# Entering values of the last state-space chunk as TensorE products with diagonal matrices

## The chip, the cores and the metric

The kernel runs on one core of a Trainium2 chip. A core has a matrix engine (TensorE, written PE in the profile; PEld is its loading of weights), a vector engine (VectorE, DVE), a scalar engine for activation functions (ScalarE, ACT), a general engine (GpSimd, POOL) and a sync engine (SP), which here issues the DMAs. Each engine works through its own queue in order, and the queues wait for each other on semaphores. SBUF is the working memory of 128 partitions. PSUM is the matrix engine's output memory, with eight banks of 128 x 512 fp32 values. The metric is the device time of one execution in microseconds (us), as the median of several runs.

## The reference

The model is a sequence of four residual layers on x of shape (2, 1024, 256): attention with ALiBi, a feed-forward layer with ternary weights, a Mamba state space, and a feed-forward layer that keeps two of every four values. The change concerns the state space, with 512 channels d, 16 states n and 128 values of low rank:

```python
x_conv = silu(conv1d(x))                       # (b, l, 512)
x_dbl = x_conv @ x_proj_weight.T               # dt_low (128), Bm (16), Cm (16)
delta = softplus(dt_low @ dt_proj_weight.T + dt_proj_bias)
deltaA = exp(einsum('bld,dn->lbdn', delta, A))
dBu = einsum('bld,bln,bld->lbdn', delta, Bm, x_conv)
h = dA * h + dbu                               # for each time l in turn
y = einsum('bdn,bn->bd', h, c)                 # then y + x_conv * D, times silu(z)
```

All values are fp32. The state h of every pair (d, n) runs through the whole sequence.

## The kernel before

Time is cut into four chunks of 512 steps, two for each of the two batch elements. A chunk goes through attention, then through the rest: `ternary_ffn`, `state_space` and `kept_two_ffn`. Python generators interleave the attention of one chunk with the rest of the chunk before it, in shares that weights after each `yield` set. The rest of the last chunk (k = 3, `tail_end` in the code) has no attention beside it and stands alone at the end. The order inside an engine's queue is made from this program by the framework's scheduler, which may move an instruction past others that do not depend on it; the tile pools add the waits for buffers that are used again.

In `state_space` a tile has 128 channels on the partitions and 512 time steps. There are four blocks of channels (c) and 16 states (n), so 64 products (c, n) per chunk. Before them, `in_proj` and the convolution make `xs`, the products `bcp` (line 531) give the 32 rows of B and C, which go through DRAM (`bcd`, line 538), and `dtl` (line 541) gives the low-rank part of delta. The input weights and these temporaries lie in the pool `mi`, which is closed before the pool `m2` of the 64 products is opened in its place.

`steps(c)` (line 552) makes delta (`dl`) and `du = delta * xs` for a block: a product `dt` on PE, Abs, Exp and Ln on ACT, `sv`, `sr` and `dl` on DVE, `sl` and `du` on POOL. It runs ahead of the loop for block 0 and in the middle of each block for the next one. The loop is a software pipeline, written as a list of stages, each with a lag (line 655). For a product i the stages are:

- `ask_b`, `ask_c` (line 582): a DMA on SP's queue spreads row n of B or C over 128 partitions (`bs`, `cs`, 256 KB each).
- `enter` (line 602): `db = du * bs`. In the last chunk DVE does this for the n that three does not divide, POOL for the others; in other chunks POOL does all.
- `decay` (line 608): `da = exp(delta * A)` on ACT. In the last chunk it goes to the two PSUM banks `s`, which attention has left free.
- `scan` (line 613): the recurrence over 512 steps on DVE, from `da`, `db` and the carried state.
- `weigh` (line 627): `hc = hs * cs` on POOL.
- `total` (line 632): four transposes by PE add hc to the bank `y` of the block; the first n adds the skip term `sk`. After the last n, `gate` (line 643) copies y, transposes it back and multiplies it by silu(z).

PSUM has two banks `s`, three `mm`, one `y` and two `r`. After the loop the out-projection `mo` (line 674) adds to x, and `kept_two_ffn` follows.

## Time and profile before

| | |
|---|---|
| median of 3 runs | 2002.48 us (2001.0 to 2005.09) |
| profiled execution, its own time | 1999.44 us |
| its span | 1997.7 us |
| busy PE, DVE, ACT, POOL | 1732.6, 1283.2, 947.2, 850.8 us |
| bytes moved by DMA | 272.73 MB |
| first scan of the last chunk starts | 1782.1 us |
| last hc of the last chunk ends | 1923.8 us |

The span is one execution from its first to its last instruction; the time of that execution lies 1.7 us above it. A group of instructions in the profile names the line, engine and operation, the tile written and the tiles read, the shape and the count; then its busy time in us and the mean of one in ns; then the idle time of the engine just before these instructions, and what ended most of it. The `[...]` in a timeline is the same for one entry. PEclk is the clock granted to PE, as a share of full speed. Matrix products are pipelined: the duration of one holds its filling and draining, and the distance between two in a row is shorter.

### The profile page before, as it was taken

What the parts mean: (1) busy time and instruction counts of PE and PEld (TensorE: products, weight loads), DVE (VectorE), ACT (ScalarE), POOL (GpSimd) and SP (SyncE); (2) the same over time, 40 slices, a digit from 0 to 9 for tenths busy, and PEclk for the clock granted to TensorE, in tenths of its full rate; (3) what the DMA queues carried; (4) which work ended last, traced back from release to release, by engine and by line L of the source; (5) the groups of instructions that cost most, each with busy time, mean ns of one, the idle gap of its engine ahead of it and who ended that gap; (6) DMA issues with size and microseconds to landing.
All of it is one profiled execution on the core that took longest, in us unless ns stands there. A gap on an engine that the chain in (4) does not pass through costs nothing.

```text
span 1997.7 us, 23402 instructions
## 1 busy us (share of the span) xinstructions
PE 1732.6 (87%) x7472; PEld 1126.7 (56%) x7472; DVE 1283.2 (64%) x2397; ACT 947.2 (47%) x1713; POOL 850.8 (43%) x690
## 2 busy tenths in 40 slices
PE   6799999798989999988879999979889999764477
PEld 4466666356656566645556576546655656523344
DVE  6865455667776474468875565567877455368964
ACT  3244464555553554455653546545544363354421
POOL 5620031467792000449992004158776000449950
PEclk9899999899999999999999999989999999875569
DMA  6333342555662313246884242256663300347740
GB/s 186 96 106 106 127 151 83 157 161 193 196 199 72 108 43 124 80 146 204 253 254 151 71 140 75 84 170 198 194 197 122 116 24 14 110 144 213 234 147 11
DMA packets 187499, 272.73 MB, mean 137 GB/s; under 512 B 17248, under 2 KB 92000, under 8 KB 186352
## 3 DMA queue, kind: packets, MB, share of 16 engines
q1 hardware_dynamic: 186224, 258.65, 41.2%
q0 software_dynamic: 1152, 12.58, 1.7%
q8 instruction: 60, 0.98, 0.2%
q14 instruction: 63, 0.52, 0.1%
HBM read 248.82 MB, written 22.35 MB: 136 GB/s over the span
## 4 chain that ended last, share of the span: by engine, by line
PE 56%; DVE 18%; POOL 11%; issue 8%; DMA 4%; ACT 3%; SPq 0%; POOLq 0%; DVEq 0%; ACTq 0%
PE z L260 10%; PE s L318 7%; DVE hs L616 6%; PE pv L298 4%; PE pq L291 4%; PE pt L249 4%; PE pk L291 4%; POOL db L606 3%; DVE ss L327 3%; POOL hc L630 3%; PE o L274 3%; PE in L501 3%; PE g_g L395 3%; PE go L738 3%; PE u_g L395 3%
## 5 line engine op out<-in xcount | busy, mean ns | idle before, releaser
L630 POOL TENSOR_TENSOR hc<-hs,cs 128x512 f32<-128x512 f32 x256 | 360.3, 1419 | 74.6 <-PE y L596 67.7
L318 PE MATMUL s<-kT,qT 128*128 128x512 f32 (+3 forms) x768 | 311.4, 514 | 28.7 <-DVE ss L322 27.4
L606 POOL TENSOR_TENSOR db<-du,bs 128x512 f32<-128x512 f32 x216 | 288.2, 1346 | 47.1 <-DVE hs L616 39.0
L331 ACT ACTIVATE ss<-ss,nm 128x128 f32<-128x128 f32 (+7 forms) x256 | 198.3, 775 | 209.4 <-DVE nm L327 202.3
L322 DVE SCALAR_TENSOR_TENSOR ss<-s,lower 128x512 f32<-128x512 f32 (+3 forms) x384 | 204.4, 550 | 141.4 <-PE s L318 141.0
L260 PE MATMUL z<-pT,v 128*128 128x512 f32 (+3 forms) x768 | 264.7, 494 | 9.8 <-ACT pT L252 9.7
L611 ACT ACTIVATE da<-dl,a_neg 128x512 f32<-128x512 f32 x256 | 175.6, 689 | 183.3 <-DVE hs L616 158.9
L596 PE MATMUL y<-ident,hc 128*128 128x128 f32 x1024 | 176.2, 315 | 93.8 <-POOL hc L630 92.8
L327 DVE CUSTOM_DVE_ANT_0 ss<-ss,alibi 128x128 f32<-128x128 f32 (+7 forms) x256 | 235.5, 926 | 2.9
L249 PE MATMUL pt<-ident,ss 128*128 128x128 f32 x1152 | 186.2, 285 | 57.8 <-DVE x L280 33.7
L260 PEld LDWEIGHTS z<-pT,v 128*128 128x128 f32 x768 | 144.9, 193 | 141.0 <-issue 100.4
L252 ACT COPY pT<-pt 128x512 f32<-128x512 f32 (+3 forms) x312 | 139.4, 470 | 178.4 <-PE pt L249 176.6
L249 PEld LDWEIGHTS pt<-ident,ss 128*128 128x128 f32 x1152 | 142.9, 146 | 116.4 <-DVE x L280 47.9
L596 PEld LDWEIGHTS y<-ident,hc 128*128 128x128 f32 x1024 | 135.9, 162 | 122.4 <-POOL hc L630 120.2
L318 PEld LDWEIGHTS s<-kT,qT 128*128 128x128 f32 x768 | 135.7, 202 | 108.0 <-issue 57.2
L616 DVE TENSOR_TENSOR_SCAN hs<-da,db 128x512 f32<-128x512 f32 x128 | 153.8, 1212 | 63.1 <-POOL hc L630 27.2
L616 DVE TENSOR_TENSOR_SCAN hs<-da,carry,db 128x512 f32<-128x512 f32 x128 | 160.2, 1271 | 18.8 <-POOL hc L630 9.5
L280 DVE SCALAR_TENSOR_TENSOR x<-o,rr,x 128x256 f32<-128x256 f32 x256 | 108.7, 477 | 62.3 <-PE o L274 62.2
L298 PEld LDWEIGHTS pv<-wv,xT_a 128*128 128x128 f32 x1024 | 124.5, 192 | 35.7 <-issue 26.0
L411 POOL DMA_DIRECT2D guT<-guT_d x4 | 2.7, 675 | 303.6 <-DVE o L743 111.9
L274 PE MATMUL o<-wo,zs 128*128 128x256 f32 x512 | 124.7, 385 | 7.4 <-ACT kT L294 6.3
L298 PE MATMUL pv<-wv,xT_a 128*128 128x128 f32 x1024 | 125.6, 276 | 4.4 <-ACT zs L265 2.3
(186 smaller groups left out, 2532.9 us busy)
## 6 DMA issues: line engine op xcount, KB each, us to landing
bs<-bcd SPq DMA_DIRECT2D x256, 256.0 KB, 4.1
cs<-bcd SPq DMA_DIRECT2D x256, 256.0 KB, 4.0
alibi<-alibi_d SPq DMA_DIRECT2D x32, 512.0 KB, 4.3
wq<-in_wqT_dram SPq DMA_DIRECT2D x64, 128.0 KB, 2.6
wk<-in_wkT_dram SPq DMA_DIRECT2D x64, 128.0 KB, 2.6
wv<-in_wvT_dram SPq DMA_DIRECT2D x64, 128.0 KB, 2.6
wo<-in_woT_dram SPq DMA_DIRECT2D x64, 128.0 KB, 2.7
alibi<-alibi_d SPq DMA_DIRECT2D x32, 256.0 KB, 3.3
```

The costliest lines, as they stand in the source:

```text
L249: nc.tensor.transpose(tp[:, i, :], s[:, (kb0 + i) * P : (kb0 + i + 1) * P], ident)
L260: nc.tensor.matmul(zp[:, q0:], lhsT=st["v_all"][:, kb, :], rhs=st["pts"][kb // 4][:, kb % 4, q0:], start=(kb == 0), stop=(kb == last),)
L274: nc.tensor.matmul(op[:, i, :], lhsT=st["z"][:, (t + i) * P : (t + i + 1) * P], rhs=st["o"], start=True, stop=True,)
L298: nc.tensor.matmul(vp[:, t, :], lhsT=xT[:, c, t * P : (t + 1) * P], rhs=st["v"][:, c, :], start=(c == 0), stop=(c == KC - 1),)
L318: nc.tensor.matmul(sp[:, :n], lhsT=st["qT"][:, j * P : (j + 1) * P], rhs=st["kT"][:, k0 : k0 + n], start=True, stop=True,)
L322: nc.vector.scalar_tensor_tensor(s[:, k0 : k0 + n], sp[:, :n], CLIP, lower[:, S - W + k0 : S - W + k0 + n], op0=ALU.min, op1=ALU.max,)
L327: nc.vector.tensor_tensor_reduce(out=s[:, :W], in0=s[:, :W], in1=st["alibi"][:, :W], scale=1.0, scalar=3.0e38, op0=ALU.add, op1=ALU.min, a ...
L331: nc.scalar.activation(s[:, :W], s[:, :W], AF.Exp, bias=nm, scale=-1.0, accum_out=st["rs"][:, j : j + 1])
L596: nc.tensor.matmul(yTs[c][:, t * P : (t + 1) * P], lhsT=h[:, t * P : (t + 1) * P], rhs=ident, is_transpose=True, start=start and t == 0, s ...
L606: mul.tensor_tensor(db[i], parts[c][1], brow.pop(i), ALU.mult)
L616: nc.vector.tensor_tensor_scan(out=hs[i], data0=da.pop(i), data1=db.pop(i), initial=0.0 if first else carry[:, n, c : c + 1], op0=ALU.mult ...
L630: nc.gpsimd.tensor_tensor(hc[i], hs.pop(i), crow.pop(i), ALU.mult)
```

## The change

In the last chunk alone, `db` is no longer an elementwise product. B is computed a second time with time on the partitions (`bT`, 128 x 4 x 16): 16 small products and a copy to SBUF. `spread_diagonal` makes, for each n, four 128 x 128 matrices whose diagonal is 128 values of B's row n: one DVE operation for even n, four ACT operations for odd n. It is called in block 0 and the matrices are kept, 32 KB per partition. `steps` transposes `du` on PE, four blocks of 128, and ACT copies the result to SBUF as `duT`. `enter_tensor` then takes, for each product and each 128 time steps, the PE product of the block of `duT` with the diagonal matrix: it gives `du * B` with channels on the partitions, in one of the three `mm` banks, from where the scan reads it. The loads of B's rows (`bs`) leave the last chunk. `da` goes to SBUF, four buffers, in place of the PSUM banks `s`. The loop calls `enter_tensor` first of its stages. Other chunks are computed as before.

```diff
--- before.py
+++ after.py
@@ -465,7 +465,6 @@
     def state_space(k):
         b, u = CH[k]
         first, last, tail_end = u == 0, u == NU - 1, k == len(CH) - 1
-        ps_da = ps_s if tail_end else ps_r
         with ExitStack() as mctx:
             mc = mctx.enter_context(tc.tile_pool(name="mc", bufs=1, side="right"))
             dt_sb = mc.tile([P, DI], F32, name=f"dt_sb_{k}")
@@ -536,6 +535,17 @@
                 nc.any.tensor_copy(bc, bc_ps[: 2 * DN, :])
                 nc.sync.dma_start(out=bcd.rearrange("a n t -> (a n) t"), in_=bc)
+                if tail_end:
+                    bT_ps = ps_r(f"bT_{k}")[:, : UT * DN].rearrange("p (t n) -> p t n", t=UT)
+                    for t in range(UT):
+                        for c in range(NDC):
+                            nc.tensor.matmul(
+                                bT_ps[:, t, :], lhsT=xs[:, c, t * P : (t + 1) * P],
+                                rhs=xp_sb[:, c, DR : DR + DN], start=(c == 0), stop=(c == NDC - 1),
+                            )
+                    bT = mc.tile([P, UT, DN], F32, name=f"bTs_{k}")
+                    nc.vector.tensor_copy(bT, bT_ps)
                 dl_ps = ps_r(f"dtl_{k}")
                 for c in range(NDC):
                     nc.tensor.matmul(
@@ -548,6 +558,18 @@
             m2 = mctx.enter_context(tc.tile_pool(name="m2", bufs=1, side="right"))
             part = lambda tag, name, bufs: m2.tile([P, U], F32, tag=tag, name=name, bufs=bufs)
             more = 2 if tail_end else 0
+            diag = m2.tile([P, DN, UT, P], F32, name=f"diag_{k}") if tail_end else None
+            def spread_diagonal(n):
+                if n % 2:
+                    for t in range(UT):
+                        nc.scalar.activation(diag[:, n, t, :], ident, AF.Copy, scale=bT[:, t, n : n + 1])
+                else:
+                    nc.vector.tensor_tensor(
+                        diag[:, n], ident.unsqueeze(1).to_broadcast([P, UT, P]),
+                        bT[:, :, n : n + 1].to_broadcast([P, UT, P]), ALU.mult,
+                    )
             def steps(c):
@@ -573,7 +595,16 @@
                 nc.vector.scalar_tensor_tensor(dl, v, 0.0, l, op0=ALU.max, op1=ALU.add)
                 du = part("du", f"du_{k}_{c}", 2)
                 nc.gpsimd.tensor_tensor(du, dl, xs[:, c, :], ALU.mult)
-                return dl, du
+                if not tail_end:
+                    return dl, du
+                tp = ps_r(f"dup_{k}_{c}")
+                for t in range(UT):
+                    nc.tensor.transpose(
+                        tp[:, t * P : (t + 1) * P], du[:, t * P : (t + 1) * P], ident
+                    )
+                duT = part("duT", f"duT_{k}_{c}", 2)
+                nc.scalar.copy(duT, tp)
+                return dl, duT
             prods = [(c, n) for c in range(NDC) for n in range(DN)]
             parts, yTs = {}, {}
@@ -588,7 +619,7 @@
                     )
                 return ask
-            ask_b, ask_c = row(brow, 0, "bs", 5 + more), row(crow, 1, "cs", 4 + more)
+            ask_b, ask_c = row(brow, 0, "bs", 5), row(crow, 1, "cs", 4 + more)
             def add(c, h, start, stop):
@@ -601,13 +632,24 @@
             def enter(i):
                 c, n = prods[i]
-                db[i] = part("db", f"db_{k}_{c}_{n}", 4 + more)
-                mul = nc.vector if tail_end and n % 3 else nc.gpsimd
-                mul.tensor_tensor(db[i], parts[c][1], brow.pop(i), ALU.mult)
+                db[i] = part("db", f"db_{k}_{c}_{n}", 4)
+                nc.gpsimd.tensor_tensor(db[i], parts[c][1], brow.pop(i), ALU.mult)
+            def enter_tensor(i):
+                c, n = prods[i]
+                if c == 0:
+                    spread_diagonal(n)
+                db[i] = ps_mm(f"db_{k}_{c}_{n}")
+                for t in range(UT):
+                    nc.tensor.matmul(
+                        db[i][:, t * P : (t + 1) * P], lhsT=parts[c][1][:, t * P : (t + 1) * P],
+                        rhs=diag[:, n, t, :], start=True, stop=True,
+                    )
             def decay(i):
                 c, n = prods[i]
-                da[i] = ps_da(f"da_{k}_{c}_{n}")
+                da[i] = part("da", f"da_{k}_{c}_{n}", 4) if tail_end else ps_r(f"da_{k}_{c}_{n}")
                 nc.scalar.activation(da[i], parts[c][0], AF.Exp, scale=a_neg[:, c, n : n + 1])
             def scan(i):
@@ -656,6 +698,9 @@
                 (5, total), (-5, ask_b), (-1, enter), (0, decay), (1, scan), (2, keep), (3, weigh),
                 (-1, ask_c),
             ]
+            if tail_end:
+                stages = [f for f in stages if f[1] not in (ask_b, enter)]
+                stages.insert(0, (-1, enter_tensor))
             for i in range(-5, len(prods) + 5):
                 if i == -1:
                     parts[0] = steps(0)
```

## The prediction

> **What bounds the kernel now.** I read the page's slices first: while the last chunk is alone, PE's clock falls to half and DVE and POOL fill up. Each column is 50 us; a digit is tenths busy, or of the full clock. Then the groups of instructions in that stretch (1782 to 1924 us).

> ```profile
> DVE  6865455667776474468875565567877455368964
> POOL 5620031467792000449992004158776000449950
> PEclk9899999899999999999999999989999999875569
> ```

> ```profile
> L630 POOL TENSOR_TENSOR hc<-hs,cs 128x512 f32<-128x512 f32 x64 | 94.3, 1494 | 1.6 <-DVE hs L616 1.6
> L616 DVE TENSOR_TENSOR_SCAN hs<-da,carry,db 128x512 f32<-128x512 f32 x64 | 79.7, 1271 | 4.9 <-POOL db L606 1.9
> L596 PE MATMUL y<-ident,hc 128*128 128x128 f32 x253 | 63.3, 406 | 70.1 <-POOL hc L630 69.2
> L606 DVE TENSOR_TENSOR db<-du,bs 128x512 f32<-128x512 f32 x39 | 46.6, 1195 | 0.0
> L611 ACT ACTIVATE da<-dl,a_neg 128x512 f32<-128x512 f32 x62 | 42.6, 690 | 77.4 <-DVE hs L616 77.3
> L606 POOL TENSOR_TENSOR db<-du,bs 128x512 f32<-128x512 f32 x23 | 31.4, 1366 | 0.0
> ```

> DVE (scan and two thirds of db) and POOL (hc and a third of db) are both 93% busy; PE and ACT mostly wait for them. The 64 scans start at 1782.08 and the last hc ends at 1923.8: 2.2 us a product. PE, which gets the work, is priced from three views: the chain of work (attention, full clock), the timeline of the stretch, and PE's busy time and clock in slices of 3.4 us.

> ```profile
> 1653.06 1.78 PE pv L298 x16
> 1659.52 1.28 PE pt L249 x10
> ```
> ```profile
> 1857.01 1.11 PE L596 MATMUL y<-ident,hc 128*128 128x128 f32 x4 [1.78 <-POOL hc L630]
> 1899.17 4.67 PE L596 MATMUL y<-ident,hc 128*128 128x128 f32 x20
> ```
> ```profile
> 963.20:966.60 3.40, 2.27 (x10) 1.00 0.95 215
> 1895.80:1899.20 3.40, 1.81 (x10) 0.50 0.84 245
> 1899.20:1902.60 3.40, 3.40 (x17) 0.50 0.82 252
> 1902.60:1906.00 3.40, 1.27 (x7) 0.87 0.85 193
> ```

> Columns of the slices: length, PE busy (records), clock, DMA share, GB/s. pv has 8 products of 128x128x128 per head and 16 records, 111 ns each: an fp32 product is two records (222 ns), a transpose one (about 108). At half clock both double.

> [...]the full slice at 1899.20 is followed by 0.87, the half-full ones stay at 0.50; once released, a slice 67% busy keeps 1.00. [...]that full slice held transposes only. [...]db on DVE takes 0.66 us alone and up to 1.76 beside POOL. The scan has one SBUF input before (db) and after (da), so I keep 1.27 us for it, 1.22 back to back ("2.45 us for 2").

> **The change, part by part.**

> *Removed.* 40 db on DVE (47 us busy), 24 on POOL (33 us), 64 row loads of 256 KB. The DMA half left, one 256 KB row per 1.3 to 1.5 us, is 175 to 200 GB/s, below the 218 moved in the stretch now: hidden, with six row buffers against 4 us to landing; without that cover each hc would wait.

> *Start of the state space.* The new order puts bT behind the last bcp product and all of dtl behind bT. bT is 16 products with 16 columns, 32 records, 26 of them behind bcp. Nearest row: ssp (128x1), 8 records in 1.05 us, so 115 ns: 26 x 0.115 = 3.0. dtl's first four records now run in a gap at 1764.13; they come later too, 1.7. dtl ends at 1769.0 + 4.7 = 1773.7. diag lies where the closed pool was, so its writers wait for dtl's last read. On ACT, 18 of the 32 diagonals stand ahead of the first Abs, which starts at 1771.68 now. [...]The nearest row, exp 128x128, has 401 ns with bias and sum; a copy of that shape 261. [...]so Abs starts at 1779.2: 7.5 later. DVE's four diagonals (0.66 each), dtl copy and dt take until 1779.0 and hide under that. Abs to first scan takes 10.4 us now. Added: two diagonals between, 0.6. From du on, now 2.3 us (one db): transposes at half clock 1.1; the duT copy behind sk, four diagonals, a table load and three exps on ACT, ready 2.4 after du; then db_0 at half clock, 8 x 0.215 + 0.25 = 2.0, and a dt product ahead of it: about 5 against 2.3, so +2.7. First scan at 1782.1 + 7.5 + 0.6 + 2.7 = 1792.9: **10.8 us late** (8 to 14). The cs rows, hc and y all wait behind it.

> *The loop, per engine.* DVE: 64 x 1.22 = 78, the steps of three further column blocks (0.75 + 0.41 + 0.68 + about 1.2 each) and three gates of 0.67: about 89. POOL: 64 hc and six step multiplications at 1.25 back to back, 87[...]. ACT: 64 x 0.65, copies and steps, under 60. PE: db is 8 x 0.111 = 0.89, y 4 x 0.108 = 0.43, so 1.32 us a product, above DVE's 1.22 and POOL's 1.25. From db_0 on: 63 x 0.89 + 58 y x 0.43 + for each further block sk, yb and dup transposes and dt, (3 x 0.43 + 0.86) x 3 = 6.5: 87.5. PE becomes the narrow bound, at full clock, since work that never stops releases it (dup, dt and db_0 to db_2 run together at the start).

> *The wait added.* PE's queue is in order, and the transposes of du for the next block stand in it ahead of further db. Block 1: du follows scan 6 by dl (1.7) and du (1.3), PE has work for 1.35: it waits 1.7. Blocks 2 and 3: sl stands behind hc_11, then dl, hc_12, du; du ends about 8.9 us after scan 9 where PE is free at 5.5: 3.4 each. Behind it stand the rest of db_14 and all y; DVE covers with scans 12 and 13 and then idles about 1.4. PE: 8.5 in all (4 to 14). The three db banks give a scan two scans' time for the next product: no wait. db now waits for the scan three before it, hc for nothing new.

> Last db at 1792.9 + 87.5 + 8.5 = 1889, its scan and hc 2.6: **1891.5 against 1923.8, 32 earlier**.

> *The end.* Now the last y, yb and the out-projection start at half clock (9.13 us for 32 records); at full clock about 2 us less there and 0.5 at y: 2.5 gained (0 to 4). Exp into SBUF: 0.69 now, 0.63 for the SBUF step exp: nothing, as ACT waits.

> *Sum.* 32 + 2.5 = 34 us, of the profiled execution's 1999.44 (span 1997.7): 1965. The median of the runs, 2002.48, stands 3 above it: **1968**. All before the last chunk has the same order of instructions.

> **The rivals.**
> A, *groups do not overlap*: if db and y, each behind its own wait, partly expose fill and drain (four y take 0.66 isolated, 0.43 in a row), a product takes about 1.55: 64 x 0.23 = 15 us less gain, 1984. Against it: y behind satisfied waits runs gapless (16 in 1.91). For it: three engines within 3 us of each other, each waiting for the others.
> B, *PE stays at half clock* (slower than before): 2.58 us a product, 87.5 more: last hc near 1979, 55 later than now, no gain at the end: about 2057. It decides from a mean clock below about 0.73 in the loop (87.5 / (1923.8 - 1792.9 - 2.6 - 8.5)). For it: PE does stand at 0.50 in this stretch. Against: the slices above.
> C, *DVE alone paces*: waits at dup vanish and the start costs 8: 1782.1 + 8 + 89 + 2.6 = 1881.7, with the end 44.5 gained: 1958.
> That the products do not land on PE is excluded by the order of instructions.

> **How the numbers follow.** Forecast 0.62, own range 1960 to 1977; A 0.18; B 0.10; C 0.10. The range takes in C's side and A with its spread: 1953 to 1992; outside lie B and the tails of A and C. 0.2% (4 us) is about what a measurement of this kernel can tell from no change. Faster: forecast, C and nearly all of A, 0.87; same 0.03 (A at full exposure, 1.8 us a product); slower 0.10, B.

> **What would show it.** In the new profile: no bs loads; PE's clock 0.9 or more through the loop; db in 512 records near 111 ns spacing; first scan near 1793; scans 1.3 to 1.5 us apart, three gaps at dup; last hc near 1891. Wrong if the clock is half for long, if the scan from PSUM takes over 1.4 us, if hc grows past 1.4[...].

## The result, and the profile after

The changed kernel takes 1980.22 us (median of 4 runs, 1978.94 to 1981.82) against 2001.74 us of the kernel before beside it: a ratio of 0.989, with a 95% interval of 0.9865 to 0.9914. It is faster, by 21.5 us where 34 were forecast. The forecast of 1968 is 12 us too low. The time lies outside the forecast's own range (1960 to 1977) and inside the whole range (1953 to 1992).

For all that follows, one execution is cut at three instants: T0 is the start of the six `bcp` records, S the start of the first scan of the last chunk, H the end of its last hc. Up to T0 the order of instructions is the same in all kernels here, and yet T0 falls between 1759.1 and 1766.3 us in their profiled executions. So lengths of stages are compared rather than instants; those of a kernel come from its one profiled execution.

| stage, us | before | forecast | after |
|---|---|---|---|
| start to T0 | 1761.4 | 1761.4 | 1762.9 |
| T0 to S | 20.6 | 31.4 | 32.0 |
| S to H (the loop) | 141.7 | 98.6 | 110.3 |
| H to the end | 73.9 | 71.4 | 71.9 |
| span | 1997.7 | 1963 | 1977.2 |

Of the missing 14 us, 11.7 lie in the loop and 1.5 ahead of T0, where nothing was changed. The page's slices of the kernel after (about 49 us each; tenths busy, or tenths of the full clock):

```profile
DVE  6865555677785473457884465667777447347754
POOL 5620022456783000429994004057778100316740
PEclk9899999899999999998999999989999999888899
```

Where the kernel before had DVE at 8 and 9 and POOL at 9 and 9 (slices 37 and 38), DVE now has 7 and 7, POOL 6 and 7; PE's clock, 5, 5 and 6 from there on, reads 8, 8 and 9. Nearly full speed, then, and still PE falls short: an average over 49 us hides why. The groups of instructions between S and H of the kernel after:

```profile
L672 POOL TENSOR_TENSOR hc<-hs,cs 128x512 f32<-128x512 f32 x64 | 83.0, 1302 | 23.5 <-DVE hs L658 21.4
L658 DVE TENSOR_TENSOR_SCAN hs<-da,carry,db 128x512 f32<-128x512 f32 x64 | 81.0, 1275 | 17.3 <-PE db L645 11.8 <-POOL hc L672 2.7 <-ACT diag L567 1.0
L645 PE MATMUL db<-diag,duT 128*128 128x128 f32 x504 | 70.5, 285 | 0.8 <-DVE hs L658 0.7
L602 PE MATMUL dup<-ident,du 128*128 128x128 f32 x12 | 3.3, 434 | 10.6 <-POOL du L597 10.6
```

Before, the hc group had idled 1.6 us; now it idles 23.5, for the scans, and the scans idle 17.3, mostly for `db`. PE is what is waited for. PE's own idle time is at `dup`: 10.6 us in three waits for du. The four `dup` behind the second wait take 1.11 us, in a window at clock 0.50; in fill (below) four take 0.66 at 1.00. The windows of PE around this wait show what comes after it. They are cut at instants 3.41 us apart, on which all changes of the clock in this trace lie (see the run `again`). After the length stand PE's busy time and records, the clock, the DMA share and GB/s:

```profile
1835.78:1839.19 3.41, 3.41 (x33) 1.00 0.50 148
1839.19:1842.60 3.41, 0.88 (x8) 1.00 0.44 147
1842.60:1846.02 3.42, 1.79 (x9) 0.50 0.26 77
1846.02:1849.43 3.41, 3.41 (x18) 0.50 0.37 77
1849.43:1852.84 3.41, 3.41 (x32) 1.00 0.29 98
```

PE does 33 records in a full window. In the next it waits from 1840.07 on and has 0.88 us of work; then follow two windows at exactly 0.50, in the second of which PE is busy throughout and gets 18 records done. In its timeline:

```profile
1844.23 1.11 PE L602 MATMUL dup<-ident,du 128*128 128x128 f32 x4 [4.16 <-POOL du L597]
1845.14 1.06 PE L645 MATMUL db<-diag,duT 128*128 128x128 f32 x4
1846.31 1.28 DVE L658 TENSOR_TENSOR_SCAN hs<-da,carry,db 128x512 f32<-128x512 f32 x1 [2.28 <-PE db L645]
1847.72 1.26 POOL L672 TENSOR_TENSOR hc<-hs,cs 128x512 f32<-128x512 f32 x1 [2.29 <-DVE hs L658]
```

du comes 4.16 us late; four `dup` and then the second half of a `db` run at half clock, the scan behind them idles 2.28 us, and hc behind the scan as long. In the loop PE is at half clock in three stretches, 3.4, 6.8 and 6.8 us long. Less the idle parts they hold 13.6 us of work, which would take 6.8 at full clock (an estimate: half the clock, twice the time; the full windows above hold 18 records at 0.50 and 32 or 33 at 1.00): **6.8 us lost** that the forecast has not priced.

Elsewhere the loop is as forecast: a product takes 1.33 us where PE doesn't wait (`db` records starting 1.33 us apart), against 1.32 forecast.

### The profile page after: what moved, and what is told of

The parts are those of the page before. It is cut to its first block, busy times and chain, and to the rows that moved or that the text cites. A ratio compares the mean times of both kernels' runs of the same rounds, so it can differ in the third digit from the quotient of the medians.

```text
span 1977.2 us, 24362 instructions
## 1 busy us (share of the span) xinstructions
PE 1769.0 (89%) x8032; PEld 1181.9 (60%) x8032; DVE 1245.5 (63%) x2367; ACT 959.1 (49%) x1748; POOL 807.5 (41%) x666
## 3 DMA queue, kind: packets, MB, share of 16 engines
q8 instruction: 64, 1.05, 0.2%
## 4 chain that ended last, share of the span: by engine, by line
PE 61%; DVE 14%; POOL 11%; issue 7%; ACT 4%; DMA 3%; SPq 0%; POOLq 0%; DVEq 0%; ACTq 0%
PE z L260 10%; PE s L318 8%; PE pv L298 4%; PE pq L291 4%; PE pk L291 4%; PE pt L249 4%; DVE hs L658 4%; POOL hc L672 4%; DVE ss L327 3%; PE o L274 3%; PE g_g L395 3%; PE go L783 3%; PE in L500 3%; PE u_g L395 3%; POOL db L636 3%
## 5 line engine op out<-in xcount | busy, mean ns | idle before, releaser
L672 POOL TENSOR_TENSOR hc<-hs,cs 128x512 f32<-128x512 f32 x256 | 350.2, 1376 | 94.1 <-PE y L627 65.1
L318 PE MATMUL s<-kT,qT 128*128 128x512 f32 (+3 forms) x768 | 308.4, 510 | 27.7 <-DVE ss L322 26.4
L636 POOL TENSOR_TENSOR db<-du,bs 128x512 f32<-128x512 f32 x192 | 254.9, 1340 | 48.1 <-DVE hs L658 38.9
L249 PE MATMUL pt<-ident,ss 128*128 128x128 f32 x1152 | 187.0, 286 | 57.1 <-DVE x L280 32.3
L249 PEld LDWEIGHTS pt<-ident,ss 128*128 128x128 f32 x1152 | 143.7, 147 | 115.0 <-DVE x L280 46.6
L627 PE MATMUL y<-ident,hc 128*128 128x128 f32 x1024 | 151.0, 282 | 26.4 <-POOL hc L672 26.3
L298 PEld LDWEIGHTS pv<-wv,xT_a 128*128 128x128 f32 x1024 | 124.4, 192 | 35.7 <-issue 26.1
L627 PEld LDWEIGHTS y<-ident,hc 128*128 128x128 f32 x1024 | 123.8, 147 | 35.2 <-POOL hc L672 32.9
L298 PE MATMUL pv<-wv,xT_a 128*128 128x128 f32 x1024 | 125.5, 275 | 4.4 <-ACT zs L265 2.2
```

Of the source, the lines that this page charges most:

```text
L249: nc.tensor.transpose(tp[:, i, :], s[:, (kb0 + i) * P : (kb0 + i + 1) * P], ident)
L298: nc.tensor.matmul(vp[:, t, :], lhsT=xT[:, c, t * P : (t + 1) * P], rhs=st["v"][:, c, :], start=(c == 0), stop=(c == KC - 1),)
L318: nc.tensor.matmul(sp[:, :n], lhsT=st["qT"][:, j * P : (j + 1) * P], rhs=st["kT"][:, k0 : k0 + n], start=True, stop=True,)
L627: nc.tensor.matmul(yTs[c][:, t * P : (t + 1) * P], lhsT=h[:, t * P : (t + 1) * P], rhs=ident, is_transpose=True, start=start and t == 0, s ...
L636: nc.gpsimd.tensor_tensor(db[i], parts[c][1], brow.pop(i), ALU.mult)
L672: nc.gpsimd.tensor_tensor(hc[i], hs.pop(i), crow.pop(i), ALU.mult)
```

## The experiments

Theory 1: PE is the pace, and each wait at `dup` costs twice, the wait and the half clock after it. Rivals: only the wait costs; or DVE and POOL hold the pace and catch up; or all of it is the start of the state space. The table has the stages of all kernels, with the period of a block (from the `dup` of block 2 to that of block 3, free of start and end); the ratio is to runs of the kernel before beside each. The diffs below are excerpts: `...` marks lines left out, and the notes behind `#` are not in the code.

| kernel | T0 to S | S to H | H to end | block | median us | ratio to before (95%) |
|---|---|---|---|---|---|---|
| before | 20.6 | 141.7 | 73.9 | | | |
| after | 32.0 | 110.3 | 71.9 | 30.8 | 1980.22 | 0.989 (0.9865 to 0.9914) |
| again | 32.8 | 110.4 | 71.9 | 30.8 | 1979.75 (one run) | |
| late | 33.7 | 102.9 | 72.3 | 26.4 | 1973.48 | 0.986 (0.9841 to 0.9879) |
| fill | 32.0 | 103.1 | 72.2 | 27.9 | 1970.02 | 0.9851 (0.9835 to 0.9866) |
| turn_b | 23.9 | 106.8 | 71.8 | 29.6 | 1968.43 | 0.984 (0.9825 to 0.9854) |
| start | 23.5 | 110.0 | 71.8 | 29.6 | 1968.57 | 0.9845 (0.9826 to 0.9865) |
| best | 23.1 | 98.8 | 71.9 | 26.4 | 1955.28 | 0.9762 (0.9736 to 0.9788) |
| best32 | 23.1 | 98.1 | 73.9 | 26.7 | 1959.26 | 0.977 (0.9738 to 0.9801) |
| da_sbuf | 20.7 | 198.5 | 74.4 | | 2059.22 (one run) | |

### fill: the wait stays, the idleness goes

```diff
                 tp = ps_r(f"dup_{k}_{c}")
...
+                        with tc.issue_after(after):        # the db product ahead of dup
+                            for m in range(2 if c == 1 else 4):
+                                busy = nc.tensor.matmul(
+                                    ps_s(f"busy_{k}_{c}_{m}"), lhsT=ident, rhs=xs[:, c, :], start=True, stop=True
+                                )
+                        o.enter_context(tc.issue_after(busy.ins))   # for dup
```

> The steps stay where they are and du comes no earlier; PE's idle time ahead of the transposes of du is filled with products that nobody reads (128x512, about 0.89 us each at full clock: two ahead of block 1's, four ahead of blocks 2's and 3's), so PE waits as long for du but isn't idle. Theory 1 (the half clock after the wait is a loss of its own): PE's clock stays at 0.95 or more through the loop, the 3.3, 5.4 and 5.3 us at half clock go, and 5 to 7 us are won: 1973 to 1975. Theory 2 (only the wait costs): the same as the changed kernel or 1 us slower, 1980.

The same place in its trace, in windows of PE, and the timeline:

```profile
1832.90:1836.31 3.41, 3.41 (x33) 1.00 0.44 119
1836.31:1839.73 3.42, 3.42 (x10) 1.00 0.33 125
1839.73:1843.14 3.41, 3.15 (x28) 1.00 0.25 85
1843.14:1846.55 3.41, 3.41 (x33) 1.00 0.56 175
```
```profile
1836.22 3.60 PE L607 MATMUL busy<-xs,ident 128*128 128x512 f32 x8
1839.67 0.66 PE L615 MATMUL dup<-ident,du 128*128 128x128 f32 x4
1840.16 1.06 PE L658 MATMUL db<-diag,duT 128*128 128x128 f32 x8
```

Four useless products fill 3.60 us, `dup` follows with no wait at 0.66 us for four instead of 1.11, and the clock is 1.00 from S to H. The loop takes 103.1 us instead of 110.3: 7.2 won. PE was hardly freer for the work that matters (the ten fillers took 9.1 us and 0.6 of waiting was left, against 10.6 of waiting): 0.9 of the 7.2 can come from that difference. So theory 1 holds: the half clock cost about as much as counted in the trace, 6.8.

The edit does one thing more: in blocks 2 and 3 `dup` now follows a whole db product, where in the changed kernel it parts one in two. That this matters little is seen in turn_b (below), where `dup` parts the product as well: a block there holds 2.9 us of work at half clock instead of 5.2. Half of the difference is 1.15 us, and the block is 1.1 us shorter (29.6 against 30.8).

### late: the wait goes too

```diff
-                if 0 <= i < len(prods) and i % DN == DN // 2 and i // DN + 1 < NDC:
+                if 0 <= i < len(prods) and i % DN == (4 if tail_end else DN // 2) and i // DN + 1 < NDC:
                     parts[i // DN + 1] = steps(i // DN + 1)
                     yield 3
+                if tail_end and 0 <= i < len(prods) and i % DN == 13 and i // DN + 1 < NDC:
+                    c = i // DN + 1
+                    parts[c] = turned(c, *parts[c], made[i + 1].ins)   # dup and duT
```

> The steps of the next column block are issued four products earlier, and the transposes of its du stand in PE's queue behind the db products of product 14 instead of in the middle of product 9 to 14's: du is there before PE comes to them. Theory 1, the wait and the half clock after it both cost, since PE is the pace: PE's waits at dup (10.6 us) shrink to under 1 us, PE keeps full clock from the first scan to the last hc, and the loop takes about 93 us instead of 110.4, the whole about 1963 (1960 to 1967). Theory 2, only the wait costs, the half clock is hidden by the banks that PE had filled ahead: about 1970. Theory 3, DVE and POOL hold the pace and catch up after each wait: 1975 or more.

No wait at `dup` is left, and a block takes 26.4 us, 4.4 less than in the changed kernel and 1.5 less than in fill. So of what a block lost, some 2.9 went with the half clock, and 1.5 more with the wait that fill had kept. The loop as a whole is only 7.4 us shorter, not 17: with the steps so early in block 1, where the diagonals are still being made, PE waits 2.1 us for a scan behind `sl` and `dl`, and the clock falls there for 3.4 us instead of at `dup`. In later blocks the first `y` now waits 1.5 us for `sk`. Of theory 1 the first half holds (both cost), its sum does not: a wait that is taken away lets the next one appear, at `sk`, and the other engines are near: in the loop DVE is busy 91.7 us and POOL 88.9 of 102.9.

### turn_b and start: the start of the state space

```diff
-                    for t in range(UT):
-                        for c in range(NDC):
-                            nc.tensor.matmul(
-                                bT_ps[:, t, :], lhsT=xs[:, c, t * P : (t + 1) * P],
-                                rhs=xp_sb[:, c, DR : DR + DN], start=(c == 0), stop=(c == NDC - 1),
-                            )
...
                 dl_ps = ps_r(f"dtl_{k}")
...
                 nc.any.tensor_copy(dtl, dl_ps)
...
+                    for t in range(UT):
+                        nc.tensor.transpose(
+                            bT_ps[:, t, :], bc[:DN, t * P : (t + 1) * P], ident[:DN, :DN]
+                        )
```

> B transposed is taken from the bc rows already in SBUF by four TensorE transposes (16 columns each) behind dtl, in place of 16 products of 16 columns ahead of it. Theory 1: dtl is back where it was in the kernel before (5 us earlier), but ACT's 18 diagonals still stand ahead of Abs: Abs some 4 us earlier, first scan near 1791, whole 1976. Theory 2, the start is set by the diagonals and the closed pool rather than by dtl: 1 us or less.

`start` moves the diagonals as well:

```diff
+                    with tc.issue_after(marks["ln"]):      # the first Ln
+                        for t in range(UT):
+                            nc.scalar.activation(diag[:, n, t, :], ident, AF.Copy, scale=bT[:, t, n : n + 1])
...
+                    with tc.issue_after(marks["sv"]):      # the first sv
+                        nc.vector.tensor_tensor(
+                            diag[:, n], ident.unsqueeze(1).to_broadcast([P, UT, P]),
+                            bT[:, :, n : n + 1].to_broadcast([P, UT, P]), ALU.mult,
+                        )
```

> As in turn_b, and the diagonals of the first products are issued behind the first block's Ln on ACT and behind the first block's sv on DVE, in the order of the queues only. Theory 1, each engine's diagonals ahead of the steps delay the first scan: first scan 1786 to 1788 instead of 1794.9, whole 1971 to 1973. Theory 2, they only move from ahead of Abs to ahead of the duT copy: no more than turn_b gives (about 1976).

T0 to S falls from 32.0 to 23.9 us in turn_b, twice what was expected. The timeline of the changed kernel, and then of turn_b:

```profile
1767.86 3.08 PE L543 MATMUL bT<-xp_sb,xs 128*128 128x16 f32 x26
1770.78 5.38 PE L551 MATMUL dtl<-xs,xp_sb 128*128 128x512 f32 x8
1776.32 5.37 ACT L567 ACTIVATE diag<-ident,bTs 128x128 f32<-128x128 f32 x18 [7.78 <-PE dtl L551]
```
```profile
1771.83 1.98 PE L540 MATMUL dtl<-xs,xp_sb 128*128 128x512 f32 x4
1776.45 0.63 ACT L583 ACTIVATE se<-sv 128x512 f32<-128x512 f32 x1 [0.29 <-DVE sv L580]
```

In the changed kernel eight `dtl` records take 5.38 us, where four take 1.98 in turn_b: the clock falls at 1770.92, right behind a window that the 16-column products of bT, for the most part, had filled to 3.41 us busy. So bT costs its own 3 us and about 1.4 more on dtl. ACT's diagonals wait for dtl too, and 18 of them stand ahead of Abs; in turn_b the scheduler puts five there and the rest later. Abs is 10.2 us behind T0, as in the kernel before. Moving the diagonals behind by hand (start) gives 0.4 us more in this stage, which is what theory 2 of start expected. Its loop is 3.2 us longer than turn_b's, with a wait of 4.46 us at the `dup` of block 1 (turn_b: 2.23) and three stretches of 3.4 us at half clock instead of two.

### again: the same kernel, another execution

> The changed kernel once more, for a second trace. Theory 1, the clock is decided at instants that lie 3.41 us apart and have nothing to do with the program, so the same wait of 4.15 us costs one or two such stretches at half clock, as it falls: the waits at dup are again near 2.3, 4.15 and 4.15 us, but the half-clock time in the loop differs from 17.1 us by 3.4 us or a multiple, and the time from the first scan to the last hc differs from 110.3 us by about half of the difference, less what of it PE idles. Theory 2, a wait of a length always costs the same: 17.1 us and 110.3 us again, within 0.5.

In each trace every change of PE's clock, at the program's start as well as 1.9 ms later, lies at a whole multiple of 3.4133 us plus one offset, within 0.01 us: offset 2.82 in the first execution of the changed kernel, 0.23 in this one, 2.24 in the kernel before. The same program had two offsets; that part of theory 1 holds. The raster fell 0.8 us later this time, and `dt` of block 0, at the same place of the program, fell into a window at clock 0.50 (two records 2.04 us instead of 1.10). First the execution shown above, then this one:

```profile
1779.46 1.10 PE L577 MATMUL dt<-dtls,dt_sb 128*128 128x512 f32 x2 [3.30 <-issue]
```
```profile
1779.40 2.04 PE L577 MATMUL dt<-dtls,dt_sb 128*128 128x512 f32 x2 [3.30 <-issue]
```

That made S come 0.75 us later behind T0. The loop moved with it, so its place on the raster changed by 0.1 us only, and it took 110.4 us with the same half-clock time. On what the raster does to the loop, this run says nothing: theory 2's numbers came out, but it wasn't a test of them. That the same wait costs one window or two is seen between kernels: 4.15 us at the `dup` of block 2 are followed by one slow window in turn_b and two in the changed kernel.

### best: both mended

turn_b and late together, but in block 1, where late had lost, the steps come at product 7.

```diff
-                if 0 <= i < len(prods) and i % DN == DN // 2 and i // DN + 1 < NDC:
+                if 0 <= i < len(prods) and i % DN == ((7 if i < DN else 4) if tail_end else DN // 2) and i // DN + 1 < NDC:
```

> turn_b, and du's transposes stand behind the db products of product 14; the steps of block 1 are issued one product earlier than in the changed kernel, those of blocks 2 and 3 four earlier. Theory 1: no wait at dup over 1 us in blocks 2 and 3, a block takes about 26.4 us there instead of 29.6, no half clock in them, the loop about 100 us instead of 106.8, the whole 1962 (1958 to 1966). Theory 2, the wait only goes elsewhere (to the first y of a block, which waits for sk, or to dl): a block takes 28 us or more, the whole 1966 or more.

One line per kernel of the stretch from S to H: before, after, best (length; PE, PEld, DVE, ACT, POOL busy and instructions; clock; DMA share; GB/s):

```profile
1782.08:1923.80 141.72, 70.90 (x280) 47.78 (x280) 131.31 (x117) 57.18 (x81) 131.94 (x93) 0.56 0.73 219
```
```profile
1794.94:1905.24 110.30, 98.70 (x796) 95.02 (x794) 90.33 (x78) 61.36 (x86) 90.21 (x70) 0.92 0.46 139
```
```profile
1782.68:1881.50 98.82, 92.94 (x796) 88.78 (x794) 89.71 (x78) 64.23 (x100) 88.70 (x70) 1.00 0.50 155
```

The clock is 1.00 over the whole loop, which takes 98.8 us, 8 less than in turn_b, of which the half-clock stretches explain some 3. The kernel takes 1955.28 us (1953.1 to 1962.32), below the expected 1958 to 1966 and 25 less than the changed kernel. The stages from T0 on give 20.5 of these 25; the rest lies ahead of T0 and in the spread of the runs. PE, DVE and POOL are busy 92.9, 89.7 and 88.7 of 98.8 us: all three are busy for about nine tenths of the loop or more.

### best32: less work for PE

```diff
-            diag = m2.tile([P, DN, UT, P], F32, name=f"diag_{k}") if tail_end else None
+            diag = m2.tile([P, DN, UT, P], F32R, name=f"diag_{k}") if tail_end else None
...
-                duT = part("duT", f"duT_{k}_{c}", 2)
+                duT = m2.tile([P, U], F32R, tag="duT", name=f"duT_{k}_{c}", bufs=2)
```

> best, with the transposed du and the diagonals held in the fp32r format, so that a db product goes through TensorE in one record instead of two[...]. Theory 1, TensorE is the pace (1.33 us a product): with db at half its time or less (0.45 us) PE has slack, DVE (1.22 to 1.27) and POOL (1.27) set the pace, and the loop shortens by 3 to 5 us against best. Theory 2, three engines are equally bound: less than 1 us.

At full clock a product now takes 1.17 to 1.26 us where products follow each other steadily (starts of `db`), instead of 1.33, so PE was the narrow bound. But the loop is only 0.7 us shorter than best's, and the end 2.0 longer. The `db` products of best and of best32, then windows of best32, the first two and four later ones, and one wait:

```profile
L650 PE MATMUL db<-diag,duT 128*128 128x128 f32 x512 | 67.3, 277 | 2.6 <-ACT duT L611 1.7 <-DVE hs L663 0.8
L650 PE MATMUL db<-diag,duT 128*128 128x128 f32 x256 | 47.1, 315 | 10.0 <-ACT duT L611 6.0 <-DVE hs L663 3.4
```

```profile
1786.25:1789.67 3.42, 2.20 (x18) 1.00 0.00 0
1789.67:1793.08 3.41, 2.66 (x11) 0.50 0.35 126
1813.54:1816.95 3.41, 1.67 (x11) 1.00 0.67 225
1816.95:1820.36 3.41, 3.41 (x16) 0.50 0.58 193
1820.36:1823.78 3.42, 1.82 (x8) 0.50 0.57 170
1823.78:1827.20 3.42, 3.42 (x18) 0.50 0.02 5
```
```profile
1823.12 1.12 PE L632 MATMUL y<-ident,sk 128*128 128x128 f32 x4 [1.54 <-ACT sk L684]
```

PE, with slack now, comes to its waits sooner and idles longer at them: 20.0 us of the loop against 5.9 in best, most of all for duT, 6.0 against 1.7, and for the copy of y (`ysb`), 5.1 against 0.1. Its clock falls: mean 0.86 over the loop against 1.00. Idle windows alone don't account for that. The window from 1816.95 is full of work (3.41 us), most of it `db`, and half clock follows all the same. The window at full clock from 1786.25 had 2.20 us of work, nearly all of it `db`, and half clock followed too; in the other kernels, windows at full clock with 1.67 us of work or more were followed by full clock, but for nine at the place of products with 1 or 16 columns (last section). Whether the format of the products has to do with it isn't shown: no run tests that alone. Theory 2's size came out, for another reason than it gave. How far the loop would shorten at full clock wasn't tried, and what the format does to the values of the result wasn't measured.

### da_sbuf: the premise of the scan's price

The kernel before, with exp writing to SBUF and nothing else changed.

```diff
-                da[i] = ps_da(f"da_{k}_{c}_{n}")
+                da[i] = part("da", f"da_{k}_{c}_{n}", 4) if tail_end else ps_r(f"da_{k}_{c}_{n}")
```

> The kernel before with one part of the change alone: exp writes its da to SBUF instead of PSUM, db stays on DVE and POOL, so the scan reads both its inputs from SBUF. Theory 1, a DVE operation with two SBUF inputs and a POOL one exclude each other (the premise on which the scan was costed unchanged, since it keeps one input in PSUM before and after the change): scans, DVE's db and POOL's work come one after the other, 64 x 1.22 + 40 x 0.66 + some 110 of POOL, about 215 us instead of 141.7, the whole 2060 to 2080. Theory 2, the place of da is of no account for the scan: 2000 to 2005.

It takes 2059.22 us, and its loop 198.5 us instead of 141.7. Groups from S to H:

```profile
L615 DVE TENSOR_TENSOR_SCAN hs<-da,carry,db 128x512 f32<-128x512 f32 x64 | 126.5, 2004 | 2.8
L629 POOL TENSOR_TENSOR hc<-hs,cs 128x512 f32<-128x512 f32 x64 | 121.8, 1922 | 8.6 <-DVE hs L615 8.6
```

Scan and hc take 2.00 and 1.92 us where they had 1.27 and 1.49; a scan beside an idle POOL (at 1904.58) still takes 1.27. So both slow down where the scan has its two inputs in SBUF and POOL works beside it. Alone, the move of `da` costs 57 us of loop; in the changed kernel, where `db` moves to PSUM with it, a scan takes 1.275 and an hc 1.30. Theory 1's full exclusion would have taken about 215 us, 16 more than measured, so exclusion isn't shown, only the slowing.

## Why the prediction was right or wrong

**Right: the kind of gain.** DVE and POOL lose `db`, 78 us of busy time, and PE becomes the narrow bound. best32 shows that PE's work per product sets the distance, and `db` and `y` together take 1.33 us where 1.32 was forecast. **The scan's price** of 1.27 us holds (1.275), and da_sbuf shows on what it hung: with `da` and `db` both in SBUF it is 2.00. **The loads** that stayed were hidden, as forecast: no hc waits for a DMA, at 139 GB/s.

**Right: rivals A and B fall.** A's 1.55 us a product is not seen. B's clock of 0.50 does not last; the mean is 0.92, above the 0.73 from which B would decide. But B was put as all or nothing, and half clock came in part.

**Wrong, the step that failed: "PE becomes the narrow bound, at full clock, since work that never stops releases it".** The next paragraph of the prediction gave PE three stops. They were priced as PE time alone, 8.5 us; nothing was put down for the clock after them. fill shows that this costs some 7 of the 11.7 us by which the loop missed (7.2 won there, 6.8 counted in the trace). The release came: the window from 1846.02, with 3.41 us of work at 0.50, was followed by 1.00. In the changed kernel's trace the clock changes on a raster of 3.41 us only, and windows with 0.88 and 1.31 us of work of 3.41, not idle ones, were followed by half clock. The prediction's slices of 3.4 us cut across these windows: its 0.87 is a slice in which the clock changed at 1903.46, from half to full, and behind that window at full clock, with 1.04 us of work, the trace of before goes back to 0.50:

```profile
1900.05:1903.46 3.41, 3.31 (x16) 0.50 0.74 202
1903.46:1906.87 3.41, 1.04 (x7) 1.00 0.92 244
1906.87:1910.29 3.42, 2.23 (x8) 0.50 0.68 210
```

**Mis-sized: the waits at `dup`.** "8.5 in all (4 to 14)" measured 10.6: 2.28, 4.16 and 4.15 us against 1.7, 3.4 and 3.4. That is 2.1 of the 11.7 us. Blocks 2 and 3 came late because dl beside a POOL multiplication took 1.74 us and waited 1.2 for sl. The last 2.4 us or so of the loop are not separated; small waits for scans in the first products and at the changes of block are in it.

**The start**: 11.4 us against 10.8. Its parts are near the forecast too: bT 3.08 us (3.0), the 18 ACT diagonals 5.37, 0.298 each (5.4, an estimate of the author's that no trace had shown), du to scan 4.7 (5.0); only dtl ended 1.0 us later, at half clock. (The 2.3 us from du to the scan in the kernel before were two `db` in a row on DVE, 2.37 us, and not one.) That bT was not needed as 16 products, and that ACT's 18 diagonals stood ahead of Abs because dtl was late, the prediction took as given; turn_b gets 8 us back.

**The end**: 2.0 against 2.5. Rival C's waits that vanish did not: each wait taken away in late uncovered another.

**The chances**: the direction came out as the likeliest case said. The time lies between the forecast's own range (1960 to 1977) and A's 1984. That the whole range holds it is partly luck: it was widened for A and C, neither of which came about, and so had room for a loss that nobody had priced.

## What to carry to other kernels

When work is moved to PE, list the waits that stand in its queue and price each twice: the wait itself (10.6 us in three here), and the work at half clock behind it (6.8 us lost here, in stretches of 3.4, 6.8 and 6.8 us). Issue what such a wait is for some products earlier (late: loop 7.4 us shorter), or put filling products ahead of it where PE has nothing better to do (fill: 7.2). Before moving a tile between PSUM and SBUF, count for each DVE operation how many of its inputs then lie in SBUF while POOL works (the scan in da_sbuf: 2.00 us with two, against 1.27 with one in the kernel before).
